# Pairs of nodes and hyperedges in 64 fixed steps on four engines

## Chip, core and metric

The kernel runs on one core of one Trainium2 chip. A core has a matrix engine (TensorE, "PE" in the profile, its weight loads "PEld"), three engines for elementwise work (VectorE "DVE", ScalarE "ACT", GpSimd "POOL") and SyncE ("SP"), which issues transfers. The engines run side by side, each in the order of its own queue, and wait for one another through semaphores. The metric is the time of the kernel on the device in microseconds (us). Before the change it is 2083.43 us, the median of three runs (2079.95 to 2089.01).

## What is computed

Four graph layers on x of 8 batches, 2048 nodes and 64 features, each of the form x = x + layer(relu(layer_norm(x))). The change lies in the first one, a hypergraph attention over 64 hyperedges. Cut to the part that matters:

```python
beta   = sigmoid((h @ a_gn)[:, None, :] + (agg @ a_ge)[:, :, None])
all_he = beta[..., None] * h[:, None, :, :] + (1.0 - beta[..., None]) * agg[:, :, None, :]
all_he = elu(all_he)                         # for every batch, hyperedge and node
coefs1 = softmax(where(H > 0, se, NEG))      # over the hyperedges of a node
g      = einsum('bne,benf->bnf', coefs1, all_he)
```

H says which hyperedge holds which node. It is sparse, so the kernel computes the mixture only for the pairs of a node and a hyperedge that exist. Afterwards g and a second candidate ("industry", made from the adjacency matrix earlier) are weighted against each other and added to x. Layers 1 to 3 follow, with products of the 2048 x 2048 adjacency.

## The kernel before

The function `layer0` first makes normalised features, tables of the hyperedges and the industry product, then the **pair stage** (L1115 to L1204), then the weighting of the two candidates (from L1210 on, called the *closing stage* below). `Layer1` and `Layers23` come after it.

The pair stage goes through 16 tiles of 128 nodes. A tile has up to 512 slots for pairs (`SLOTS`), taken as `NB` = 4 blocks of 128. So there are 64 blocks, and each handles all 8 batches at once: 128 pairs x 512 columns (8 batches x 64 features).

`begin(i)` (L1120) prepares tile i. ScalarE and VectorE make `sT`, ones and zeros that say which slot belongs to which node (L1125, L1126). A product with `Q` gives `px`, and a comparison on VectorE gives `oT`, which slot belongs to which hyperedge (L1130). Four transposes of `sT` on TensorE land in `pts`, and ScalarE copies them to `S` (L1133, L1135). Twelve small products `pm` (16 columns, L1140 to L1142) and two ScalarE operations give `be` (the gate) and `wt` (the weight) of every pair.

`pairs_of(i, k)` (L1149) handles block k. TensorE makes `pd` with three products and `pa` with one. VectorE makes `mix` = (be + 1) * pd (L1162) and adds `pa` (L1165). ScalarE takes an exponential into `ex` (L1166). VectorE combines the two (L1167), GpSimd multiplies by `wt` (L1168), and TensorE sums the pairs of a node into `pgs` (L1169, a float32 product that the profile counts as two instructions).

`end(i)` (L1171) divides by the sum of the weights on VectorE (`gn`, L1173), transposes back on TensorE (`ptg`, L1177) and stores the result from ScalarE in `gT`, whose buffer is called `hn` (L1179).

The features of a tile (`hhi` and `hlo`, 264 KB each) are loaded by GpSimd's queue two tiles ahead (`features`, L799 and L800). In tiles 0 to 11 that queue also issues one load of 1 MB of the adjacency (`aT`, L1918).

What sets the order: the kernel is written in a framework with a planner, which arranges the instructions of each engine by a simulated time of its own. In the pair stage nothing is pinned, so the planner's order holds. Elsewhere an instruction can be pinned behind the one traced before it on its engine: `InOrder(tc, engine)` (L622) does so for every call through it, and `kit.mm` and `kit.turn` (L724, L730) do it while `kit.strict` is set.

In layer 1, `scores` (L1447) loads rows `R` that VectorE needs in `attend`; the load is issued by SyncE's queue (L1453).

Of the kernel before, what the change touches and what calls it, by code (L numbers as in the profile page):

```python
# [8 lines left out]
FP = mybir.dt.float32  # L9
FR = mybir.dt.float32r  # L10
AF = mybir.ActivationFunctionType
OP = mybir.AluOpType
# [4 lines left out]
P = 128  # L17
B, N, F = 8, 2048, 64
E = 64
NP = B // 2  # L20
NT = N // P
# [10 lines left out]
def cols(c, w=CW):  # L32
    return slice(c * w, (c + 1) * w)
# [583 lines left out]
SLOTS, NB = 512, 4  # L617
HN = N // 2
# [16 lines left out]
class Kit:  # L635
# [88 lines left out]
    def mm(self, *args, **kw):  # L724

        one = self.nc.tensor.matmul(*args, **kw)  # L726
        if self.strict:
            self.tc.keep_in_program_order(one)

    def turn(self, dst, src):  # L730

        one = self.nc.tensor.transpose(dst, src, self.ident)
        if self.strict:
            self.tc.keep_in_program_order(one)
# [27 lines left out]
def layer0(kit, hn, x1_dram, open_early, late_tile, between):  # L762
# [5 lines left out]
    tc, nc, t = kit.tc, kit.nc, kit.t  # L768
    mm = nc.tensor.matmul
    ident, ones, bad = kit.ident, kit.ones, kit.bad  # L770
# [6 lines left out]
    neg1 = w0.tile([P, 1], FP, name="neg1")  # L777
# [8 lines left out]
    Q = lst.tile([P, NT, 2, E], FR, name="Q")  # L786
    slot = lst.tile([P, SLOTS], FP, name="slot")
    mid = lst.tile([P, NT], FP, name="mid")
    width = lst.tile([P, NT], FP, name="width")
    tab = lst.tile([P, B, F], FR, name="tab")  # L790
    ntab = lst.tile([P, B, F], FR, name="ntab")
    etab = lst.tile([P, 2 * B], FR, name="etab")
    rden = lst.tile([P, NT, B], FP, name="rden")

    def features(i):

        hi = lst.tile([P, B * F + 2 * B], FR, tag="hhi", name="hhi", bufs=3)
        lo = lst.tile([P, B * F + 2 * B], FR, tag="hlo", name="hlo", bufs=3)
        nc.gpsimd.dma_start(out=hi, in_=hi_dram[i].bitcast(FR))  # L799
        nc.gpsimd.dma_start(out=lo, in_=lo_dram[i].bitcast(FR))  # L800
        return hi, lo

    with ExitStack() as sA:
# [78 lines left out]
        with ExitStack() as s1:  # L882
            pool = s1.enter_context(tc.tile_pool(name="rank", bufs=1, reuse_waits="tile"))
            sb = s1.enter_context(tc.tile_pool(name="nf_sb", bufs=2, reuse_waits="tile"))
            ps = s1.enter_context(tc.tile_pool(name="nf_ps", bufs=2, space=PSUM, reuse_waits="tile"))
# [28 lines left out]
        with ExitStack() as s1:  # L914
            sp = s1.enter_context(tc.tile_pool(name="streamf", bufs=6, reuse_waits="tile"))
            sb = s1.enter_context(tc.tile_pool(name="e_sb", bufs=2, reuse_waits="tile"))
            ps = s1.enter_context(tc.tile_pool(name="e_ps", bufs=1, space=PSUM, reuse_waits="tile"))
# [4 lines left out]
            pg = ps.tile([P, B, F], FP, tag="pg", name="pg")  # L922
# [171 lines left out]
            last = None  # L1094
# [18 lines left out]
    gT = hn  # L1113
    with ExitStack() as s0:

        hot = s0.enter_context(tc.tile_pool(name="s_hot", bufs=2, reuse_waits="tile"))
        sb = s0.enter_context(tc.tile_pool(name="s_sb", bufs=2, reuse_waits="tile"))
        ps = s0.enter_context(tc.tile_pool(name="s_ps", bufs=1, space=PSUM, reuse_waits="tile"))

        def begin(i):  # L1120
            hi, lo = loaded.pop(0)

            sT = hot.tile([P, SLOTS], FR, tag="sT", name="sT")
            tmp = hot.tile([P, SLOTS], FP, tag="tmp", name="tmp", bufs=1)
            nc.scalar.activation(tmp, slot, AF.Abs, bias=mid[:, i : i + 1])  # L1125
            nc.vector.tensor_scalar(sT, tmp, width[:, i : i + 1], None, op0=OP.is_lt)  # L1126
            px = ps.tile([P, SLOTS], FP, tag="px", name="px", bufs=2)
            mm(px, Q[:, i].rearrange("p h e -> p (h e)"), sT, start=True, stop=True)
            oT = hot.tile([P, SLOTS], FR, tag="oT", name="oT")
            nc.vector.tensor_tensor(oT, px, slot, op=OP.is_equal)  # L1130
            pt = ps.tile([P, NB, P], FP, tag="px", name="pts", bufs=2)
            for k in range(NB):
                nc.tensor.transpose(pt[:, k, :], sT[:, k * P : (k + 1) * P].bitcast(FP), ident)  # L1133
            S = sb.tile([P, NB, P], FP, tag="S", name="S")
            nc.scalar.copy(S, pt)  # L1135

            pm = ps.tile([P, NB, 2 * B], FP, tag="px", name="pm", bufs=2)
            for k in range(NB):
                ks = slice(k * P, (k + 1) * P)
                mm(pm[:, k, :], sT[:, ks], hi[:, B * F :], start=True, stop=False)  # L1140
                mm(pm[:, k, :], sT[:, ks], lo[:, B * F :], start=False, stop=False)
                mm(pm[:, k, :], oT[:, ks], etab, start=False, stop=True)  # L1142
            be = sb.tile([P, NB, B], FP, tag="be", name="be")
            wt = sb.tile([P, NB, B], FP, tag="wt", name="wt")
            nc.scalar.activation(be, pm[:, :, 0:B], AF.Tanh, scale=0.5)
            nc.scalar.copy(wt, pm[:, :, B:])
            return hi[:, 0 : B * F], lo[:, 0 : B * F], sT, oT, S, be, wt

        def pairs_of(i, k, pg, hi, lo, sT, oT, S, be, wt):  # L1149
            ks = slice(k * P, (k + 1) * P)  # L1150
            flat = lambda a: a.rearrange("p b f -> p (b f)")
            pd = ps.tile([P, B, F], FP, tag="pd", name="pd", bufs=2)
            mm(flat(pd), sT[:, ks], hi, start=True, stop=False)
            mm(flat(pd), sT[:, ks], lo, start=False, stop=False)
            mm(flat(pd), oT[:, ks], flat(ntab), start=False, stop=True)
            pa = ps.tile([P, B, F], FP, tag="pa", name="pa", bufs=2)
            mm(flat(pa), oT[:, ks], flat(tab), start=True, stop=True)
            mix = sb.tile([P, B, F], FP, tag="mix", name="mix", bufs=3)
            ex = sb.tile([P, B, F], FP, tag="ex", name="ex", bufs=3)


            nc.vector.scalar_tensor_tensor(  # L1162
                mix, be[:, k, :, None].to_broadcast([P, B, F]), 1.0, pd, op0=OP.add, op1=OP.mult
            )
            nc.vector.tensor_tensor(mix, mix, pa, op=OP.add)  # L1165
            nc.scalar.activation(ex, mix, AF.Exp, bias=neg1)  # L1166
            nc.vector.scalar_tensor_tensor(ex, mix, 1.0, ex, op0=OP.max, op1=OP.min)  # L1167
            nc.gpsimd.tensor_tensor(mix, ex, wt[:, k, :, None].to_broadcast([P, B, F]), op=OP.mult)  # L1168
            return lambda: mm(flat(pg), S[:, k, :], flat(mix), start=k == 0, stop=k == NB - 1)  # L1169

        def end(i, pg):  # L1171
            gn = sb.tile([P, B, F], FP, tag="gn", name="gn")
            nc.vector.tensor_tensor(gn, pg, rden[:, i, :, None].to_broadcast([P, B, F]), op=OP.mult)  # L1173
            pt = ps.tile([P, NP, P], FP, tag="px", name="ptg", bufs=2)
            gf = gn.rearrange("p b f -> p (b f)")
            for p in range(NP):
                nc.tensor.transpose(pt[:, p, :], gf[:, p * P : (p + 1) * P], ident)  # L1177
            for p in range(NP):
                nc.scalar.activation(gT[p][:, i * P : (i + 1) * P], pt[:, p, :], AF.Identity, bias=neg1)  # L1179

        now = begin(0)

        for p in range(1, NP):
            nc.sync.dma_start(out=x1_dram[p], in_=t["xT"][p])
        late = None
        for i in range(NT):
            pg = ps.tile([P, B, F], FP, tag="pg", name="pgs")
            todo = []
            for k in range(NB):
                todo.append(pairs_of(i, k, pg, *now))  # L1190
                if k == 1 and i + 1 < NT:
                    after = begin(i + 1)
                if k == 2:
                    if i + 2 < NT:
                        loaded.append(features(i + 2))
                    load_early(i)
                if k == 1 and late is not None:
                    late()
                if k > 0:
                    todo[k - 1]()  # L1200
            todo[-1]()
            now = after
            late = lambda i=i, pg=pg: end(i, pg)
        late()  # L1204

    sP.close()
    one = between(None)
# [90 lines left out]
class Layer1:  # L1298
# [148 lines left out]
    def scores(self, p, hf, b2):  # L1447

        self.turn += 1
        r = (self.sb2 if self.turn % 3 == 0 else self.R).tile([P, HN], FP, tag="R", name="R", bufs=2 - (self.turn % 3 == 0))  # L1450
        if b2 is None:
            return r
        self.kit.nc.sync.dma_start(out=r, in_=self.r_dram[p, b2 : b2 + 1, cols(hf, HN)].to_broadcast([P, HN]))  # L1453
        return r

    def attend(self, aT, p, hS, vd, wd, hf, between):
# [98 lines left out]
class Weave:  # L1555
# [9 lines left out]
    def step(self, c):  # L1565
        d = next(c[1], None)
        if d is None:
            self.chains.remove(c)
        else:
            c[0] = self.now + d  # L1570
# [419 lines left out]
```

## Time and profile before

| | us |
|---|---|
| median of three runs | 2083.43 |
| profiled execution, its own time | 2082.92 |
| its span in the profile | 2081.0 |
| up to the pair stage | 0 to 246 |
| pair stage | 246 to 442.3 |
| closing stage of layer 0 | 442.3 to 521 |
| layer 1 | 521 to 938 |
| layers 2 and 3 | 938 to 2081 |

The profiled execution took 1.9 us more than its span and 0.5 us less than the median of the runs. Over the span TensorE is busy 96%, VectorE 58%, ScalarE 22% and GpSimd 13%. These are averages over stages with different limits. Busy time of TensorE also counts the draining of each product, so that a busy TensorE can still have room.

In a timeline or table of groups, a line gives the line of the kernel, engine, operation, the tile written and those read, and after the bar (or in square brackets) the idle time before it and what ended it.

### The profile page before, as it was taken

What the parts mean: (1) busy time and instruction counts of PE and PEld (TensorE: products, weight loads), DVE (VectorE), ACT (ScalarE), POOL (GpSimd) and SP (SyncE); (2) the same over time, 40 slices, a digit from 0 to 9 for tenths busy, and PEclk for the clock granted to TensorE, in tenths of its full rate; (3) what the DMA queues carried; (4) which work ended last, traced back from release to release, by engine and by line L of the source; (5) the groups of instructions that cost most, each with busy time, mean ns of one, the idle gap of its engine ahead of it and who ended that gap; (6) DMA issues with size and microseconds to landing.
All of it is one profiled execution on the core that took longest, in us unless ns stands there. A gap on an engine that the chain in (4) does not pass through costs nothing.

```text
span 2081.0 us, 23594 instructions
## 1 busy us (share of the span) xinstructions
PE 2005.6 (96%) x9164; PEld 1154.1 (55%) x9164; DVE 1196.8 (58%) x1882; ACT 455.5 (22%) x859; POOL 264.2 (13%) x383
## 2 busy tenths in 40 slices
PE   7999899887999999999999999999999999999997
PEld 4777655533322222227775557765477755577653
DVE  6667478976888888883224653225632156522355
ACT  4321244457112121112121111211111211112100
POOL 0211054422000000000001210002100012100022
PEclk9999899999999999999999999999999999999999
DMA  6666272157111111213200012101022000121000
GB/s 180 195 193 190 67 239 80 43 154 162 46 42 35 49 33 23 60 31 89 66 31 21 25 37 60 58 7 35 18 64 61 26 22 25 37 75 46 8 14 12
DMA packets 84251, 138.16 MB, mean 66 GB/s; under 512 B 32753, under 2 KB 33009, under 8 KB 81457
## 3 DMA queue, kind: packets, MB, share of 16 engines
q1 hardware_dynamic: 65200, 83.86, 13.7%
q0 software_dynamic: 18928, 52.70, 10.2%
q8 instruction: 74, 1.21, 0.2%
q14 instruction: 49, 0.39, 0.1%
HBM read 102.64 MB, written 37.03 MB: 67 GB/s over the span
## 4 chain that ended last, share of the span: by engine, by line
PE 68%; issue 15%; DVE 6%; POOL 4%; DMA 3%; ACT 2%; SPq 0%; POOLq 0%; DVEq 0%; ACTq 0%
PE acc L726 27%; PE o L726 11%; PE u L726 6%; PE dn L726 5%; PE acc L940 3%; PE pgs L1169 2%; PE var L726 2%; PE mean L726 2%; PE py L726 2%; POOL fold L1878 1%; DVE ex L1167 1%; DMA at<-in_adjT 1%; PE ph L726 1%; POOL ot L1879 1%; DMA iv<-ind_dram 1%
## 5 line engine op out<-in xcount | busy, mean ns | idle before, releaser
L726 PE MATMUL acc<-aT,parts 128*128 128x512 f32 x1664 | 456.0, 420 | 0.0
L726 PEld LDWEIGHTS acc<-aT,parts 128*128 128x128 f32 x1664 | 307.8, 188 | 111.8 <-issue 49.4
L1866 DVE TENSOR_TENSOR pr<-u,embf 128x512 f32<-128x512 f32 x256 | 170.7, 688 | 138.8 <-PE u L726 131.9
L1485 DVE SCALAR_TENSOR_TENSOR pt<-R,wd,aT 128x1024 f32<-128x1024 f32 x192 | 236.5, 1279 | 20.4 <-PE dn L726 6.6
L726 PE MATMUL u<-W3f,y 64*128 64x512 f32 x1024 | 241.0, 589 | 0.0
L726 PE MATMUL o<-pt,hS 128*64 128x512 f32 x1024 | 236.4, 599 | 3.0 <-DVE pt L1485 3.0
L726 PEld LDWEIGHTS u<-W3f,y 64*128 64x128 f32 x1024 | 99.2, 187 | 120.6 <-issue 120.6
L726 PEld LDWEIGHTS o<-pt,hS 128*64 128x64 f32 x1024 | 68.0, 136 | 161.4 <-issue 149.9
L940 PE MATMUL acc<-at,Y 128*128 128x512 f32 x512 | 137.0, 413 | 2.4 <-DVE ev L949 2.4
L726 PE MATMUL u<-W3f,v 64*128 64x512 f32 x512 | 138.8, 619 | 0.0
L726 PE MATMUL dn<-pt,vd 128*32 128x512 f32 x1024 | 123.1, 598 | 0.0
L1702 DVE TENSOR_TENSOR yb<-py,cb_f 128x512 f32<-128x512 f32 x32 | 22.1, 691 | 173.7 <-PE py L726 173.7
L1878 POOL TENSOR_TENSOR fold<-fold 128x256 f32<-128x256 f32 x64 | 47.7, 745 | 548.4 <-DVE fold L1877 510.6
L940 PEld LDWEIGHTS acc<-at,Y 128*128 128x128 f32 x512 | 95.8, 195 | 25.7 <-issue 4.3
L726 PE MATMUL acc<-aTl,parts 128*128 128x512 f32 x384 | 103.2, 405 | 0.0
L1870 DVE TENSOR_TENSOR pr<-pr 128x512 f32<-128x512 f32 x128 | 88.1, 688 | 2.2
L1485 DVE SCALAR_TENSOR_TENSOR pt<-R,wd,aTl 128x1024 f32<-128x1024 f32 x64 | 79.8, 1282 | 11.4 <-PE dn L726 8.2
L726 PEld LDWEIGHTS acc<-aTl,parts 128*128 128x128 f32 x384 | 72.2, 188 | 21.5 <-issue 5.7
L1169 PE MATMUL pgs<-mix,S 128*128 128x512 f32 x128 | 69.8, 635 | 13.1 <-POOL mix L1168 12.4
L1852 ACT COPY xs<-px 128x128 f32<-128x128 f32 x64 | 17.1, 267 | 272.7 <-POOL ot L1880 210.3
L1168 POOL TENSOR_TENSOR mix<-ex,wt 128x512 f32<-128x512 f32 x64 | 66.7, 1042 | 76.7 <-DVE ex L1167 66.4
L1770 POOL TENSOR_TENSOR bq<-bq,xp 128x512 f32<-128x512 f32 x16 | 20.5, 1283 | 434.1 <-DVE xp L1768 395.5
(321 smaller groups left out, 2672.8 us busy)
## 6 DMA issues: line engine op xcount, KB each, us to landing
at<-in_adjT POOLq DMA_DIRECT2D x32, 512.0 KB, 4.6
raw<-in_adjT SPq DMA_DIRECT2D x64, 256.0 KB, 3.4
aT<-in_adjT POOLq DMA_DIRECT2D x12, 1024.0 KB, 6.1
xp<-xd SPq DMA_DIRECT2D x45, 256.0 KB, 3.2
R<-r_dram SPq DMA_DIRECT2D x14, 512.0 KB, 3.8
hi_dram<-hi SPq DMA_DIRECT2D x16, 264.0 KB, 2.4
lo_dram<-lo SPq DMA_DIRECT2D x16, 264.0 KB, 3.4
hhi<-hi_dram POOLq DMA_DIRECT2D x16, 264.0 KB, 3.0
```

What stands on the lines that cost most here:

```text
L726: one = self.nc.tensor.matmul(*args, **kw)
L940: mm(acc[p], Y[h][:, m, p, :], at[:, k, :], start=m + h == 0, stop=m == NT - 1 and h == 1)
L1167: nc.vector.scalar_tensor_tensor(ex, mix, 1.0, ex, op0=OP.max, op1=OP.min)
L1168: nc.gpsimd.tensor_tensor(mix, ex, wt[:, k, :, None].to_broadcast([P, B, F]), op=OP.mult)
L1169: return lambda: mm(flat(pg), S[:, k, :], flat(mix), start=k == 0, stop=k == NB - 1)
L1485: nc.vector.scalar_tensor_tensor(pt, R[b2], wd[:, m, b2 : b2 + 1], aT[m][:, s].bitcast(FP), op0=OP.max, op1=OP.mult)
L1702: nc.vector.tensor_tensor(yb, py, bias[:, None, :].to_broadcast([P, 4, P]), op=OP.add)
L1770: nc.gpsimd.tensor_add(bq, bq, xp)
L1866: nc.vector.tensor_tensor(a, u[h], emb[:, i, 8 * w : 8 * w + 8, None].to_broadcast([P, 8, F]), op=OP.mult)
L1870: nc.vector.tensor_add(pr[h], pr[h], a)
L1878: nc.gpsimd.tensor_add(fold[:, :, 0:2, :], fold[:, :, 0:2, :], fold[:, :, 2:4, :])
L1879: nc.gpsimd.tensor_add(ot, fold[:, :, 0, :], fold[:, :, 1, :])
```

## The change

The pair stage is written anew. The parts of `begin`, `pairs_of` and `end` become small functions. A loop of 64 + 7 steps calls them so that each operation is written two or more steps behind its operands. VectorE, ScalarE, GpSimd and TensorE are pinned to the order of the text in this loop.

Apart from the order:

- the comparison that makes `sT` moves from VectorE to GpSimd;
- the four transposes of `sT` become products with a copy of the identity (`ident_r`) in the type that TensorE takes rounded (float32r), as `sT` is;
- more buffers: `sT` 3 instead of 2, `S` 3 instead of 2, `mix` 6 instead of 3, `ex` 4 instead of 3, and `pgs` in PSUM 2 instead of 1;
- in layer 1, the loads of `R` for the last pair of batches are pinned behind what was traced before them on SyncE's queue.

```diff
+        V, A, G = InOrder(tc, nc.vector), InOrder(tc, nc.scalar), InOrder(tc, nc.gpsimd)
...
-            nc.vector.tensor_scalar(sT, tmp, width[:, i : i + 1], None, op0=OP.is_lt)
+            G.tensor_scalar(d["sT"], tmp, width[:, i : i + 1], None, op0=OP.is_lt)
...
-                nc.tensor.transpose(pt[:, k, :], sT[:, k * P : (k + 1) * P].bitcast(FP), ident)
+                mm(d["pt"][:, k, :], d["sT"][:, k * P : (k + 1) * P], ident_r, start=True, stop=True)
...
+        for step in (nodes, ranks, edges, turn, turned, shares, shared):
+            step(0)
+        nodes(1)
...
+        for j in range(last + 7):
+            i, k = divmod(j, NB)
+            there = i + 1 < NT
+            if j < last:
+                pairs_of(j)
+            if k == 2 and i + 2 < NT:
+                nodes(i + 2)
+            if 1 <= j <= last:
+                mixed(j - 1)
+            if 3 <= j < last + 3:
+                weighed(j - 3)
+            if 5 <= j < last + 5:
+                gathered(j - 5)
+            if k == 0:
+                if there:
+                    ranks(i + 1)
+                if i > 2:
+                    done(i - 3)
+            if k == 1:
+                if there:
+                    turn(i + 1)
+                    edges(i + 1)
+                if i > 1:
+                    divided(i - 2)
+            if k == 2:
+                if there:
+                    turned(i + 1)
+                    shares(i + 1)
+                if i + 2 < NT:
+                    loaded.append(features(i + 2))
+                if i < NT:
                     load_early(i)
+                if i > NT:
+                    back(i - 2)
+                    done(i - 2)
+            if k == 3:
+                if 1 < i <= NT:
+                    back(i - 2)
+                if there:
+                    shared(i + 1)
...
+        if p == NP - 1:
+
+            self.kit.tc.keep_in_program_order(one)
```

The functions by engine: `nodes` makes `sT` (ScalarE, GpSimd). `ranks` makes `px` (TensorE) and `edges` makes `oT` (VectorE). `turn` writes `pts` (TensorE) and `turned` copies it to `S` (ScalarE). `shares` makes `pm` (TensorE), and `shared` makes `be` and `wt` (ScalarE). `mixed` holds the two VectorE operations and the exponential of a block. `weighed` is the third VectorE operation and GpSimd's product, `gathered` the sum into `pgs`. `divided`, `back` and `done` are the three parts of `end`.

## The prediction

> **What bounds the kernel now.** I read the stages first: busy time of each engine in five stretches of the span. Columns: stretch, its length, busy us (and instructions) of PE, PEld, DVE, ACT, POOL, then TensorE's granted clock, DMA share, GB/s.
>
> ```profile
> 246.00:442.30 196.30, 173.83 (x724) 111.58 (x726) 163.87 (x244) 84.76 (x191) 87.27 (x103) 0.95 0.36 111
> 442.30:521.00 78.70, 65.44 (x263) 24.41 (x260) 53.04 (x80) 56.37 (x77) 14.99 (x19) 0.95 0.83 198
> ```
>
> The pair stage takes 196.3 us with TensorE and VectorE both near 85% busy; the rest of the kernel hardly concerns the change. Successive starts of `gn`, once per tile, run from 273.9 to 439.2 us: 165.3 / 15 = 11.02 us per tile, 11.42 in the middle. Four tiles there (362.81 to 408.49 us) I took apart by groups, shapes separate:
>
> ```profile
> L1169 PE MATMUL pgs<-mix,S 128*128 128x512 f32 x32 | 17.4, 625 | 4.7 <-POOL mix L1168 4.5
> L1168 POOL TENSOR_TENSOR mix<-ex,wt 128x512 f32<-128x512 f32 x16 | 16.7, 1043 | 14.9 <-DVE ex L1167 14.8
> L1167 DVE SCALAR_TENSOR_TENSOR ex<-mix,ex 128x512 f32<-128x512 f32 x16 | 14.1, 879 | 3.8 <-ACT ex L1166 3.8
> L1165 DVE TENSOR_TENSOR mix<-mix,pa 128x512 f32<-128x512 f32 x16 | 10.9, 681 | 0.3
> L1162 DVE SCALAR_TENSOR_TENSOR mix<-be,pd 128x512 f32<-128x512 f32 x16 | 10.9, 681 | 0.1
> L1126 DVE TENSOR_SCALAR sT<-tmp,width 128x512 fp32r<-128x512 f32 x4 | 2.9, 715 | 0.0
> ```
>
> VectorE idles only 5.0 us of 45.68 (3.8 + 0.3 + 0.1 + 0.8 before `oT`), so it is occupied (45.68 - 5.0) / 4 = 10.17 us per tile. TensorE waits for GpSimd's product, GpSimd for VectorE's `ex`, VectorE for ScalarE's exponential: one block's chain, walked with little else to do. The waits of the same stretch, longest first, say it directly (columns: total us, times, longest):
>
> ```profile
> POOL mix L1168 <- DVE ex L1167: 14.8, 12, 3.0
> PEld pgs L1169 <- POOL mix L1168: 9.0, 10, 1.4
> ```
>
> Two timelines give the real pitch. A busy VectorE starts an operation every 0.60 us though each lasts 0.68, but 0.71 behind one whose result it reads (here 367.74 to 368.45):
>
> ```profile
> 367.74 0.68 DVE L1162 SCALAR_TENSOR_TENSOR mix<-be,pd 128x512 f32<-128x512 f32 x1
> 368.45 0.69 DVE L1165 TENSOR_TENSOR mix<-mix,pa 128x512 f32<-128x512 f32 x1
> 369.06 0.69 DVE L1167 SCALAR_TENSOR_TENSOR ex<-mix,ex 128x512 f32<-128x512 f32 x1
> 369.66 0.68 DVE L1162 SCALAR_TENSOR_TENSOR mix<-be,pd 128x512 f32<-128x512 f32 x1
> 370.26 1.22 DVE L1167 SCALAR_TENSOR_TENSOR ex<-mix,ex 128x512 f32<-128x512 f32 x1
> ```
>
> The last line is an `ex` that took 1.22 us: GpSimd's product ran then. On TensorE:
>
> ```profile
> 384.14 0.39 PE L1154 MATMUL pd<-hlo,sT 128*128 128x512 f32 x1
> 384.37 0.39 PE L1155 MATMUL pd<-ntab,oT 128*128 128x512 f32 x1
> 384.60 1.02 PE L1169 MATMUL pgs<-mix,S 128*128 128x512 f32 x2
> 385.06 0.80 PE L1157 MATMUL pa<-tab,oT 128*128 128x512 f32 x1
> 385.69 0.39 PE L1153 MATMUL pd<-hhi,sT 128*128 128x512 f32 x1
> ```
>
> A product of 512 columns costs 0.23 us, a `pgs` that needn't wait 385.69 - 384.60 - 0.23 = 0.86 us.
>
> **What the Trainium skill says.** GPSIMD Engine Reference, 1. Specifications: GpSimd's SBUF interfaces are shared with VectorE, with "contention with DVE instructions in a 2-port perf mode or with two SBUF inputs". The trace agrees: `ex`, with two SBUF inputs, has mean 879 and up to 1700 ns, the operations that read PSUM stay at 681. The same page, 3.1, gives 769 ns for a 512-element loop with one input on GpSimd; no such row is in this trace. Perfetto Trace Analysis, Identifying the Most-Contended Engine: matmul busy share is no measure of distance to the limit; hence the pitches above. TensorE: Matmul & The Clock Gate, Part 1: half clock after an idle window; the trace shows 0.56 from 256 to 267 us.
>
> **The change part by part.** VectorE per tile: `sT` leaves (0.72). What stays is 4 x (0.71 + 0.60 + 0.60) + `oT` 0.60 + `gn` 0.60 = 8.84 us. Holds by GpSimd are now (879 - 682) x 4 = 0.79. In the new order GpSimd's product (1.04) starts as `ex` ends, and VectorE's next `ex` comes 1.31 us later, behind two operations that read PSUM, so they should hardly meet; bounds 8.84 to 9.63.
>
> TensorE per tile: 16 x 0.23 = 3.68; `pgs` 4 x 0.86 = 3.44; `px` 0.23; twelve `pm` 1.34 (382.49 to 383.83 us); `ptg` 0.44 (376.41 to 376.85). Sum 9.13. `pts` as rounded products isn't in the trace: as cheap as now, 0.44, or each as dear as a 512-column product, 0.92. So 9.57 to 10.05; I take 9.8, in the middle.
>
> GpSimd per tile: 4 x 1.04 + two or three DMA issues of 0.57 + `sT`. For that I take an estimate of 0.8 us from the skill's 769 ns; bounds 0.5 (an iota of 512 took 0.55) and 1.3 (the 512-wide addition of L1770). Sum about 6.7, no bound. `sT` stands two steps, some 5 us, before the `px` that reads it; with ScalarE's part its chain is 1.5 us long. On GpSimd only the product of the same step is queued behind it. ScalarE: 4 x 0.73 + 1.14 + 0.59 + 0.72 + 0.38 = 5.75, no bound.
>
> So TensorE sets the pace. Does something else stop it? With TensorE at 2.5 us a step, VectorE starts step j when `pd` of j-1 is written, 1.0 us into TensorE's step j-1. So the `ex` of block j-5, VectorE's third operation of step j-2, ends 1.0 + 1.9 = 2.9 us after TensorE began step j-3, and GpSimd's product 1.2 later. TensorE asks for it 0.9 us into step j, 3 x 2.5 + 0.9 = 8.4 us after that beginning. Some 4 us are spare, which also cover the 2.2 to 2.7 us that GpSimd's queue now loses before some `hhi` loads. The tightest are the two PSUM buffers shared by `px`, `pts`, `pm` and `ptg`: `turn` waits for four ScalarE copies written one step before, with some 1.8 us spare. For uneven steps (the one with `pm` 1.3 us longer, VectorE's with `oT` and `gn` 1.2) and semaphores I add an estimated 0.3. Tile: 10.1 us.
>
> Stage: the first `mix` starts at 251.9 us now; GpSimd's slower `sT` and the identity copy add about 1: 253. Then 63 steps x 10.1 / 4 = 159.1. The clock dip stays: 10.3 us busy at 0.56 lose 4.5. Drain behind the last `mix`: 1.31 + 0.73 + 0.69 + 1.05 + 1.25 + 0.69 + 0.44 + 1.14 + waits 0.5 = 7.8. End at 424.4 instead of 442.3: 17.9 us less.
>
> After it everything moves along. At 442 three accumulating stores (1 MB each) and seven `iv` loads fill the transfers, and one `iv` lands 18.7 us late; they start when the last tile is done and its buffers are free, in both kernels. More buffers change only which tile `iv` overlays: nothing, give or take 3.
>
> R: at 831 us three loads (512 KB each) go out together, and VectorE waits 0.80 and 1.22 us for two of them. Pinned, the third goes later, behind the two loads `xp` that SyncE issues at 836.7 us and one that follows them; its rows are needed only in the second half of that pair, half of 836 to 938 us on; two share the transfers. Between 0 and 2 us gained, I take 1.
>
> Sum: 17.9 + 1 = 19 us from the profiled 2082.9: 2064; the median of the runs stood 0.5 higher: 2064.5.
>
> **Rivals.** *VectorE and GpSimd still collide* (holds of 0.8 plus waits in the tight PSUM ring): tile near 10.85, 63 / 4 x 10.85 = 170.9, 11.8 more than mine: 2076. For it: VectorE's slack against TensorE is under 1 us; against: ten of fourteen operations read PSUM.
>
> *Slower: the fixed order makes GpSimd's operations fall on every `ex`.* `sT` and the DMA issues push the product back until it covers the next `ex`; a hold has cost up to 1.70 - 0.69 = 1.0. Four per tile: 9.2 + 4.0 = 13.2, 63 / 4 x 3.1 = 49 us over mine: 2113. It decides from 2.7 us of holds per tile on: 9.2 + 2.7 = 11.9, the stage is then 10 us longer than now. Against: the alternation mends itself, as a late product delays TensorE, not `ex`.
>
> *The gain is swallowed in the closing stage*: the planner issues `iv` or the stores in a worse order; the stretch with DMA share 0.83 is 78.7 us long, a tenth of it lost is 8: 2073.
>
> *Better still*: the dip of the clock goes as well, and 9.6 per tile: 4.5 + 7.9 less, 2052.
>
> **How the numbers follow.** Mine 0.66 (own range 2055 to 2074), collision 0.14, slower 0.11, swallowed 0.06, better 0.03. Runs of this kernel spread by 0.4%, so 0.5% (10.4 us) is what can be told from no change: faster means under 2073. Faster takes mine, better and half of swallowed, less a margin: 0.75; same 0.15 (collision); slower 0.10. The range 2053 to 2084 leaves out the slower case, its own lower end apart, and a part of better.
>
> **What would show it.** `gn` every 10.1 us; hardly any wait of `pgs` for GpSimd; mean `ex` below 750 ns; no `sT` on VectorE, a GpSimd row of 0.5 to 1.3 us; `pts` starting 0.11 to 0.23 us apart; the stage over by 424; the closing stage still 79 us. Wrong if the waits of TensorE move to `pts` or `px` (the PSUM ring), if `ex` stays near 880, or if a step waits for GpSimd's queue behind an `hhi` load.

## The result and the profile after

The changed kernel takes 2055.03 us (median of 4 runs, 2053.27 to 2057.83), the kernel before 2086.22 us in the same session. The ratio is 0.9857, with a 95% interval of 0.9834 to 0.9881. Forecast were 2064.5 us and a range of 2053 to 2084. The profiled execution took 2053.27 us, its span 2051.2; before these were 2082.92 and 2081.0.

To see where the 29.8 us of span went, I cut both spans at the same events. The first column ends where VectorE makes the reciprocal degrees just ahead of the pair stage, the second with the last copy to `hn`, the third with the first `pt` of layer 1, the fourth with its last `ds`.

| us | up to the pair stage | pair stage | closing stage | layer 1 | layers 2 and 3 |
|---|---|---|---|---|---|
| before | 244.7 | 197.7 | 78.6 | 417.3 | 1142.7 |
| after | 241.7 | 169.1 | 82.3 | 415.2 | 1142.9 |
| difference | -3.0 | -28.6 | +3.7 | -2.1 | +0.2 |

So the pair stage gave nearly everything. The first and third columns also move where no edit reaches: over the kernels below, with the same code ahead of the pair stage, the first runs from 235.4 to 250.6 us, and the closing stage, where its code is that of the changed kernel, from 79.1 to 86.1. So the 3.0 us less and the 3.7 us more are within what these stages scatter. The pair stage repeats: three traces with the same code in it (the changed kernel and two of those below) give 169.1 us each. I judge edits by it.

The stages by busy time, after (same columns as before: stretch, length, PE, PEld, DVE, ACT, POOL, granted clock, DMA share, GB/s):

```profile
246.00:410.50 164.50, 160.16 (x718) 112.21 (x719) 148.77 (x228) 82.35 (x190) 112.21 (x117) 0.97 0.44 131
410.50:495.40 84.90, 68.76 (x272) 25.88 (x269) 54.35 (x82) 58.65 (x81) 15.34 (x19) 0.92 0.82 189
```

TensorE is now busy 160.2 of 164.5 us. Four tiles in the middle, 282.34 to 320.68 us, take 38.34 us, so 9.58 each. Their groups:

```profile
L630 POOL TENSOR_TENSOR mix<-ex,wt 128x512 f32<-128x512 f32 x16 | 17.0, 1063 | 4.6 <-DVE ex L630 4.4
L726 PE MATMUL pgs<-mix,S 128*128 128x512 f32 x32 | 16.3, 592 | 0.0
L630 DVE SCALAR_TENSOR_TENSOR ex<-mix,ex 128x512 f32<-128x512 f32 x17 | 12.7, 749 | 0.0
L630 DVE TENSOR_TENSOR mix<-mix,pa 128x512 f32<-128x512 f32 x17 | 11.7, 688 | 1.8
L630 POOL TENSOR_SCALAR sT<-tmp,width 128x512 fp32r<-128x512 f32 x5 | 7.8, 1560 | 0.0
```

Pinned operations all carry the helper's line, L630 or L726, and are told apart by their tiles. The 4.7 us that `pgs` stood idle in four tiles are now 0.0. VectorE's 3.8 us ahead of `ex` are 0.0, and GpSimd's wait for `ex` fell from 14.8 to 4.4. `sT` on GpSimd takes 1.56 us, twice what I had taken.

What changed shows best in the chain, followed back to what released each piece (columns: start, length, what). One block of the kernel before goes from engine to engine:

```profile
363.40 0.63 ACT ex L1166
364.05 1.71 DVE ex L1167
365.90 1.05 POOL mix L1168
366.99 1.12 PE pgs L1169 x2
```

After, a whole tile is TensorE alone, and the next tile begins where it ends:

```profile
291.92 1.24 PE pm L726 x12
293.16 0.79 PE pd L726 x3
293.95 0.23 PE pa L726
294.18 0.86 PE pgs L726 x2
295.04 0.44 PE ptg L732 x4
295.48 0.69 PE pd L726 x3
...
297.26 0.23 PE px L726
297.49 0.69 PE pd L726 x3
...
299.28 0.39 PE pts L726 x4
299.67 0.76 PE pd L726 x3
...
301.51 1.24 PE pm L726 x12
```

From 340 us on a tile takes 9.85, and the piece that grew is the one whose buffers I had called the tightest. The chain again, then the waits of 340.12 to 379.53 us (total, times, longest):

```profile
357.35 0.64 PE pts L726 x4
```

```profile
PEld pts L726 <- ACT hn L630: 3.3, 4, 0.8
```

`pts` takes 0.64 instead of 0.39, since it waits for ScalarE's copies of the tile before to free the PSUM buffer. That costs 0.27 us in each of five tiles, 1.3 us in all.

### The profile page after: what moved, and what is told of

Same layout as the page of the kernel before. It is cut to its first block, busy times and chain, and to the rows that moved or that the text cites. A ratio compares the mean times of both kernels' runs of the same rounds, so it can differ in the third digit from the quotient of the medians.

```text
span 2051.2 us, 23618 instructions
## 1 busy us (share of the span) xinstructions
PE 1992.0 (97%) x9164; PEld 1153.7 (56%) x9164; DVE 1184.3 (58%) x1867; ACT 454.4 (22%) x859; POOL 291.4 (14%) x399
## 3 DMA queue, kind: packets, MB, share of 16 engines
q1 hardware_dynamic: 65200, 83.86, 13.9%
## 4 chain that ended last, share of the span: by engine, by line
PE 71%; issue 15%; POOL 4%; DVE 3%; DMA 3%; ACT 2%; SPq 0%; POOLq 0%; DVEq 0%; ACTq 0%
PE acc L726 28%; PE o L726 11%; PE dn L726 6%; PE u L726 6%; PE pd L726 3%; PE acc L940 3%; PE pgs L726 2%; PE var L726 2%; PE mean L726 2%; PE py L726 2%; POOL fold L1964 1%; DMA iv<-ind_dram 1%; PE pm L726 1%; POOL ot L1965 1%; PE ph L726 1%
## 5 line engine op out<-in xcount | busy, mean ns | idle before, releaser
L726 PE MATMUL acc<-aT,parts 128*128 128x512 f32 x1664 | 456.0, 419 | 0.0
L726 PEld LDWEIGHTS acc<-aT,parts 128*128 128x128 f32 x1664 | 307.8, 188 | 111.8 <-issue 49.4
L726 PE MATMUL u<-W3f,y 64*128 64x512 f32 x1024 | 241.0, 589 | 0.0
L726 PE MATMUL o<-pt,hS 128*64 128x512 f32 x1024 | 236.4, 599 | 0.8 <-DVE pt L1571 0.6
L726 PEld LDWEIGHTS u<-W3f,y 64*128 64x128 f32 x1024 | 99.2, 187 | 120.6 <-issue 120.6
L726 PEld LDWEIGHTS o<-pt,hS 128*64 128x64 f32 x1024 | 68.0, 136 | 159.2 <-issue 150.2
L726 PE MATMUL u<-W3f,v 64*128 64x512 f32 x512 | 138.8, 619 | 0.0
L726 PE MATMUL dn<-pt,vd 128*32 128x512 f32 x1024 | 123.1, 598 | 0.0
L726 PE MATMUL acc<-aTl,parts 128*128 128x512 f32 x384 | 103.1, 405 | 0.0
L726 PEld LDWEIGHTS acc<-aTl,parts 128*128 128x128 f32 x384 | 72.2, 188 | 21.5 <-issue 5.7
L630 POOL TENSOR_TENSOR mix<-ex,wt 128x512 f32<-128x512 f32 x64 | 68.3, 1069 | 33.7 <-DVE ex L630 28.9
L726 PEld LDWEIGHTS dn<-pt,vd 128*32 128x32 f32 x1024 | 26.7, 108 | 80.8 <-issue 75.4
```

Of the source, the lines that this page charges most:

```text
L630: self.tc.keep_in_program_order(getattr(self.engine, name)(*args, **kw))
```

## The experiments

My theory, A in the records, is that the gain comes from distance: each engine finds its operands ready since they were asked for steps ago, and a fixed order keeps it so. The rivals credit one part instead, such as the comparison moved off VectorE, the extra buffers or the products in place of transposes. Not everything stands two steps behind its operands, as the section on the change has it: `mix` is one step behind `pd`, the exponential stands in the step of its sum, and GpSimd's product in that of its `ex`. Two steps lie between the exponential and `ex`, and two between the product and `pgs`. The measured stage lengths stand against 169.1 us of the changed kernel and 197.7 us of the kernel before.

**The shortest distance**: `ex` stands in the step of its exponential, and the sum one step later.

```diff
-            if 3 <= j < last + 3:
-                weighed(j - 3)
-            if 5 <= j < last + 5:
-                gathered(j - 5)
+            if 1 <= j < last + 1:
+                weighed(j - 1)
+            if 2 <= j < last + 2:
+                gathered(j - 2)
```

> The kernel after, with ex combined in the same step as its exponential is asked for and the sum into pgs one step later. Everything else of the change stays (pins, buffers, sT on GpSimd, pts as products). Theory A: VectorE now waits some 0.8 us for ScalarE in each of 64 steps, a step takes near 3.0 us and a tile 13.0, so the stage is about 50 us longer: 2095 to 2110. Theory B: VectorE's work is as small as in the kernel after, 2054 to 2065.

Measured: 2110.56 us, ratio to before 1.0124 (1.0095 to 1.0154), pair stage 225.4 us. With every other edit in place, the shorter distance costs 56 us and makes the kernel slower than the one before. VectorE's timeline shows what comes back (start, length, engine, line, operation, and in brackets the idle time before it):

```profile
322.01 0.69 DVE L630 SCALAR_TENSOR_TENSOR ex<-mix,ex 128x512 f32<-128x512 f32 x1 [0.86 <-ACT ex L630]
322.62 0.68 DVE L630 SCALAR_TENSOR_TENSOR mix<-be,pd 128x512 f32<-128x512 f32 x1
323.40 0.69 DVE L630 TENSOR_TENSOR mix<-mix,pa 128x512 f32<-128x512 f32 x1
324.94 0.69 DVE L630 SCALAR_TENSOR_TENSOR ex<-mix,ex 128x512 f32<-128x512 f32 x1 [0.85 <-ACT ex L630]
```

VectorE stands 0.85 us in every block for the exponential of its own last sum. A block takes it 324.94 - 322.01 = 2.93 us, and with `oT` and `gn` a tile takes 4 x 2.93 + 2 x 0.6 = 12.9 us. Starts of `gn` are 12.93 us apart up to 339 us and up to 13.9 later, where TensorE's clock dips. That is near the 13.2 of my slower rival, but by another mechanism: the rival had `ex` held by GpSimd, and here `ex` has a mean of 733 ns in 305 to 375 us.

**One step less for `ex`, two for the sum**

```diff
-            if 3 <= j < last + 3:
-                weighed(j - 3)
-            if 5 <= j < last + 5:
-                gathered(j - 5)
+            if 2 <= j < last + 2:
+                weighed(j - 2)
+            if 3 <= j < last + 3:
+                gathered(j - 3)
```

> The kernel after, with ex combined two steps behind pairs_of instead of three and the sum into pgs three steps behind instead of five. Theory A by its own count: some 4 us are spare, two steps less take 5 us of distance and VectorE's move gives 2.5 back, so 1 to 2 us stay spare: same time within 3 us, 2052 to 2058. If every step of distance is needed (GpSimd's queue with sT and loads delays products by more than that): pgs waits for mix again, 2060 to 2075.

Measured: 2052.64 us, 0.9863 (0.9825 to 0.9900), pair stage 169.3. There was slack to spare, as counted, but not much more: in 305 to 375 us `pgs` waits 1.3 us for GpSimd again. Here as at the shortest distance the sum stands one step behind the product. What differs is whether `ex` stands in the step of its exponential or one later, and that alone is worth 56 us.

**No pins.** The text, the distances and the buffers stay; the planner may arrange.

```diff
-        V, A, G = InOrder(tc, nc.vector), InOrder(tc, nc.scalar), InOrder(tc, nc.gpsimd)
+        V, A, G = nc.vector, nc.scalar, nc.gpsimd
...
-        kit.strict = True
         last = NB * NT
```

> The kernel after without any pin in the pair stage (the pin of R stays): text, buffers, sT on GpSimd and pts as products are those of the kernel after, the planner orders. Theory A: most of the gain goes, 2070 to 2085, with pgs waiting for GpSimd's mix as before. Theory B, or the buffers as the cause: the gain stays, 2053 to 2062.

Measured: 2061.77 us, 0.9895 (0.9868 to 0.9922), pair stage 172.6. Only 3.5 of 28.6 us go, as Theory B had it. The second half of my theory falls: a fixed order isn't needed for most of the gain, since the planner keeps close to a text in which operations already stand apart. What the pins still save shows where its tiles are slow (timelines of GpSimd, ScalarE and TensorE):

```profile
345.85 2.08 POOL L1134 TENSOR_SCALAR sT<-tmp,width 128x512 fp32r<-128x512 f32 x1
```

```profile
347.96 0.72 ACT L1133 ACTIVATE tmp<-slot,mid 128x512 f32<-128x512 f32 x1 [3.47 <-POOL sT L1134]
348.59 0.86 ACT L1234 ACTIVATE hn<-ptg,neg 128x128 f32<-128x128 f32 x3
```

```profile
350.37 0.66 PE L726 MATMUL pts<-ident_r,sT 128*128 128x128 f32 x4 [0.66 <-ACT hn L1234]
```

The planner has put the next tile's `tmp` right behind `sT`, whose one input buffer it overwrites. ScalarE stands 3.47 us, the copies to `hn` are queued behind it, and TensorE's `pts` waits for those. `pts` of five successive tiles starts at 328.98, 339.82, 350.37, 360.91 and 371.44 us: 10.6 us a tile where the changed kernel takes 9.9, which is 2.8 us over these four.

**The buffers alone, in the order of before** (`sT`, `S`, `mix`, `ex` and `pgs` get the numbers of the changed kernel):

```diff
-            mix = sb.tile([P, B, F], FP, tag="mix", name="mix", bufs=3)
-            ex = sb.tile([P, B, F], FP, tag="ex", name="ex", bufs=3)
+            mix = sb.tile([P, B, F], FP, tag="mix", name="mix", bufs=6)
+            ex = sb.tile([P, B, F], FP, tag="ex", name="ex", bufs=4)
```

> The kernel before with the buffer counts of the kernel after (sT 3, S 3, mix 6, ex 4, pgs 2) and nothing else. Theory A: the planner's order keeps the chains, at most 5 us are gained: 2077 to 2086. Theory C (buffers as the cause): 2055 to 2065.

Measured: 2073.09 us, 0.9963 (0.9952 to 0.9975), pair stage 187.4. Buffers alone give 10.3 of 28.6 us, between the theories. In 335 to 405 us `ex` falls from 869 to 686 ns, so it is no longer held; but `sT` on VectorE rises from 715 to 974 ns, and the wait of GpSimd for `ex` grows from 23.4 to 29.6 us. Freeing `ex` without the order leaves the chain of one block.

**The move of `sT` alone, in the order of before**

```diff
-            nc.vector.tensor_scalar(sT, tmp, width[:, i : i + 1], None, op0=OP.is_lt)
+            nc.gpsimd.tensor_scalar(sT, tmp, width[:, i : i + 1], None, op0=OP.is_lt)
```

> The kernel before with sT made on GpSimd and nothing else. Theory A: VectorE loses 0.7 us per tile, GpSimd gets 1.56 us in front of products that are waited for; between 5 us gained and 10 lost: 2077 to 2093. Theory B: 0.7 us x 16 = 11 us or more gained: 2060 to 2072.

Measured: 2094.93 us, 1.0065 (1.0046 to 1.0084), pair stage 207.6. That is a little beyond what Theory A allowed. The edit that helps in the new order costs 9.9 us in the old one. GpSimd's timeline, TensorE's and the busy time of the 4 us that follow tell why (the last with the columns of the stages above):

```profile
355.61 2.12 POOL L1126 TENSOR_SCALAR sT<-tmp,width 128x512 fp32r<-128x512 f32 x1
357.63 0.59 POOL L800 DMA_DIRECT2D hlo<-lo_dram  x1
358.24 1.06 POOL L1168 TENSOR_TENSOR mix<-ex,wt 128x512 f32<-128x512 f32 x1
```

```profile
359.36 1.61 PE L1169 MATMUL pgs<-mix,S 128*128 128x512 f32 x2 [2.22 <-POOL mix L1168]
```

```profile
359.40:363.40 4.00, 4.00 (x9) 2.67 (x10) 2.58 (x4) 1.33 (x3) 1.50 (x2) 0.57 0.18 54
```

The product's `ex` was ready at 356.33 us, but the product starts at 358.24, queued behind `sT` and a load. TensorE stands 2.22 us for it, and in the 4 us after that its clock is 0.57: the delay is paid twice. It happens once per tile from 345 to 414 us, six times in all, with waits of 2.21 to 2.24 us.

**The order and the buffers alone, and each of the other two edits with them.** `sT` back on VectorE:

```diff
-            G.tensor_scalar(d["sT"], tmp, width[:, i : i + 1], None, op0=OP.is_lt)
+            V.tensor_scalar(d["sT"], tmp, width[:, i : i + 1], None, op0=OP.is_lt)
```

> The kernel after, with sT made on VectorE again. Theory A (the distance between an operation and its operands lets TensorE run without waits; TensorE's own products set the pace): VectorE has about 9.2 of 9.6 us per tile in use and takes 0.5 to 0.7 us back, so it comes to 9.7 to 9.9, about as long as TensorE's tile: 2054 to 2060 us, ex with a mean near 700 ns. Theory B (VectorE's load was the limit, and the gain is sT and the holds that leave it): 0.7 to 1.5 us per tile come back, 2065 to 2078 us.

Transposes in place of products:

```diff
-                mm(d["pt"][:, k, :], d["sT"][:, k * P : (k + 1) * P], ident_r, start=True, stop=True)
+                kit.turn(d["pt"][:, k, :], d["sT"][:, k * P : (k + 1) * P].bitcast(FP))
```

> The kernel after with pts as four transposes against the float32 identity again. Four starts of pts are 0.11 us apart in the kernel before; in the kernel after the group of four takes about 0.50 us to the next product against 0.44. Nothing measurable: within 2 us of the kernel after, 2052 to 2057. If the product form mattered as much as its upper bound in the prediction, 8 us faster.

Both of these edits at once:

> The kernel after with sT on VectorE and pts as transposes, as in the kernel before: only the order, the buffers and the pin of R are left of the change. The two single runs lost 4.1 and 3.6 us in the pair stage, both with longer waits at pts. If they add: 169.1 + 7.7 = 177 us; if both are the same wait: 173. In either case the order and its buffers carry 20 us or more of the 28.6: 2058 to 2068 in all. If the gain needs the three together: 185 us or more, 2072 and up.

| | time, us | ratio to before | pair stage, us | lost of 28.6 |
|---|---|---|---|---|
| `sT` on VectorE | 2062.37 | 0.9893 (0.9863 to 0.9923) | 173.2 | 4.1 |
| transposes | 2059.73 | 0.9909 (0.9889 to 0.9928) | 172.7 | 3.6 |
| both | 2060.35 | 0.9903 (0.9876 to 0.9931) | 172.7 | 3.6 |

Both single runs fell outside what I had put first (2054 to 2060 and 2052 to 2057). Order and buffers give 25.0 of 28.6 us without the other two edits. Each of those is worth nothing without the other, and together they are worth 3.6. The chains show why: with `sT` on VectorE it is VectorE, not TensorE, that carries the chain through the middle of the stage (here with `sT` on VectorE and the products kept).

```profile
331.53 0.60 DVE ex L630
332.13 0.60 DVE oT L630
...
333.25 0.48 DVE sT L630
333.72 0.61 DVE mix L630
```

Eight tiles there take 81.2 us: two take 9.56 each, the other six 10.35 on average. By the prediction's own count VectorE needs 8.84 + 0.72 = 9.56 with `sT`, and `ex` at a mean of 854 ns, where I had put it near 700, adds (854 - 682) x 4 = 0.69. So the edits to TensorE's work can't help there. With the transposes and `sT` on GpSimd, TensorE starts with the same 9.58 us and then, in five tiles, takes 10.30; the chain passes ScalarE's copies:

```profile
357.15 0.72 ACT ex L630
357.87 1.03 ACT hn L630 x4
...
358.95 0.66 PE pts L732 x4
```

This is the PSUM ring again, only worse than in the changed kernel. Why transposes make it worse isn't settled: where nothing waits, four of them and the three `pd` behind them take 0.44 + 0.69 us in the chain, the products and their `pd` 0.39 + 0.76, which is the same.

**The PSUM wait taken away.** The copies to `hn` are placed ahead of the step's exponential:

```diff
+            if k == 0 and i > 2:
+                done(i - 3)
             if 1 <= j <= last:
                 mixed(j - 1)
...
-                if i > 2:
-                    done(i - 3)
```

> The kernel after, with done (the four ScalarE copies out of ptg) ahead of the exponential in the steps with k = 0; in the last steps nothing changes. In the kernel after the tiles from 340 us on wait 0.7 us each at pts for these copies and take 9.85 us, those from 282 to 321 us don't and take 9.59. Theory A with the shared PSUM buffers as what is left: that wait goes, all tiles near 9.6, 2 to 4 us less in the pair stage (167 us or less, from the comparison of VectorE's rdeg to the last copy, against 169.1). If the wait has another cause, it stays. The whole kernel: 2050 to 2056.

Measured: 2055.03 us, 0.9868 (0.9842 to 0.9894), pair stage 168.6. The wait of `pts` is gone and tiles stay at 9.58 to 9.69 us. The stage shrinks by 0.5 us, less than the 1.3 that five tiles had lost and far less than the 2 to 4 on record, and the whole time doesn't move. The cause of the wait was the one named, its size small.

**The pin on `R` taken away**

```diff
-        if p == NP - 1:
-
-            self.kit.tc.keep_in_program_order(one)
```

> The kernel after without the pin of the R loads in layer 1. From the two traces layer 1 took 417.3 us before and 415.2 after, so 2 us come back: 2055 to 2058, with three R loads at the start of the last pair. If the planner's shifted clock, not the pin, changed that place: no difference.

Measured: 2063.44 us, 0.9916 (0.9901 to 0.9931); layer 1 takes 416.3 us instead of 415.2. The three loads go out together again, at 797 us. Over layer 1 the waits for `R` are 6.4 us without the pin, 5.2 with it and 6.2 before. The other traces agree: layer 1 takes 414.6 to 415.4 us in the ten with the pin and 415.6 to 417.3 in the four without. So the pin is worth about 1 us. The whole time, beyond the range on record, can't show it: the profiled execution of this kernel took 2048.08 us and the timed ones 2062.7 to 2064.3, with the same pair stage of 169.1 us in the trace.

**The closing stage.** It is 3.7 us longer than before. Its chain passes one `iv` load; first the kernel before, then the changed one:

```profile
442.97 18.68 DMA iv<-ind_dram
```

```profile
411.88 20.93 DMA iv<-ind_dram
```

I took this load for the cause. It is not shown to be one. With `sT` on VectorE it takes only 18.24 us, and the stage 86.0. Nor do TensorE and ScalarE stand still meanwhile, as the record below has it: in these 20.9 us they are busy 17.5 and 13.6 us with other chunks (columns as in the stages above).

```profile
411.88:432.81 20.93, 17.46 (x60) 5.50 (x60) 13.99 (x19) 13.61 (x15) 1.41 (x2) 0.92 1.00 237
```

Three `iv` loads were fetched ahead of the end of the pair stage, and the three 1 MB stores placed later and pinned:

```diff
         first(0)
         kit.strict = False
         first(1)
+        for i in range(2, 5):
+            fetch(i)
...
-            if i in (1, 4, 8):
-                p = 1 + i // 4
-                nc.gpsimd.dma_start(out=x1_dram[p], in_=gT[p], accum_op=OP.add)
+            if i in (5, 9, 13):
+                p = i // 4
+                tc.keep_in_program_order(nc.gpsimd.dma_start(out=x1_dram[p], in_=gT[p], accum_op=OP.add))
```

> The kernel after, with two edits behind the pair stage: three of the iv loads are issued before the loads of xo, and the three 1 MB accumulating stores of hn stand at later places (steps 5, 9 and 13 of the closing stage instead of 1, 4 and 8) and are pinned there on GpSimd's queue. In the kernel after TensorE and ScalarE stand still from 412 to 433 us, until an iv load lands 20.9 us after its issue among those stores. If the stores are what delays it: it lands after some 5 us, the closing stage takes 65 to 70 us instead of 82, 2038 to 2045 in all. If the closing stage is bound by the sum of its transfers: no gain, 2050 to 2056.

The same together with the earlier copies to `hn`:

> The last two edits together (done ahead of the exponential; stores late): the gains add, 2036 to 2043. Nothing of the computation is left out.

Measured: 2050.41 us, 0.9853 (0.9827 to 0.9880), closing stage 77.0; and together 2053.76 us, 0.9871 (0.9847 to 0.9895), closing stage 77.2. The longest `iv` piece left in the chain is this:

```profile
420.68 2.72 DMA iv<-ind_dram
```

The load of 20.9 us is gone from the chain, the stage only 5 us shorter (2 us below the shortest of the others), well under the gain on record in both runs. The waits of that stage in the first of the two kernels:

```profile
POOL aTl L2010 <- DVE iv L630: 27.0, 1, 27.0
...
PEld pf L726 <- ACT th_s L630: 14.0, 16, 5.2
...
PEld pd L726 <- DVE iv L630: 11.4, 14, 1.5
```

The second and third are waits of TensorE for ScalarE and VectorE, chunk by chunk, and the changed kernel had them too (11.9 and 12.6 us): beside the load ran a chain that is nearly as long. GpSimd's 27.0 us ahead of an `aTl` load were 24.5 in the changed kernel; what they cost isn't isolated. No version here is shown to beat the changed kernel: the intervals of all the near ones overlap with its own.

Not tried: the new order with the old buffers. Buffers alone gave 10.3 us and order and buffers 25.0, so the order adds 14.7 on top of them; what it is worth without them stays open.

## Why the prediction was right or wrong

Direction, mechanism and bound were right: TensorE sets the pace, the chain of one block is gone, and the time lies in the range. The gain was under-sized, 29.8 us of span against 19. That 2055.03 us still falls at the very edge of my own range (2055 to 2074) is partly luck: the drain and the scatter of the closing stage took back 6.1 us of what the steps gave beyond my sum. By the prediction's own terms:

| term | forecast, us | measured, us | effect on the end |
|---|---|---|---|
| first `mix` | 253 | 250.3 | -2.7 |
| 63 steps and the clock dip | 159.1 + 4.5 | 150.3 | -13.3 |
| drain behind the last `mix` | 7.8 | 10.2 | +2.4 |
| end of the pair stage | 424.4 | 410.8 | -13.6 |
| closing stage | 78.6 | 82.3 | +3.7 |
| layer 1 | -1 | -2.1 | -1.1 |

**The tile is where it was mis-sized.** I took TensorE's work as 9.8, the middle of 9.57 to 10.05, and added 0.3 for uneven steps and semaphores. Measured were 9.58 in the first half and 9.85 later. The chain of a tile above gives the terms: `pm` 1.24 (forecast 1.34), `ptg` 0.44, `px` 0.23, `pgs` 4 x 0.86, all products `pd` and `pa` 3.86 (3.68) and `pts` 0.39 (0.44 to 0.92). So the rounded `pts` are no dearer than the transposes had been, and taking the middle put 0.2 too much. The allowance of 0.3 was the larger error: TensorE took its uneven steps without a wait, since its operands lay ready. The 0.5 us too many per tile make 63 / 4 x 0.5 = 7.9 us, as the rival *better still* had it.

**The clock dip** I put down as staying at 256 to 267 us, during the steps, with 4.5 us lost. It is now at 246 to 256 (clock 0.52); in 256 to 267 the clock is 1.00. Part of it lies ahead of the first `mix` at 250.3. Behind it TensorE is busy some 4.6 us at half clock, an estimated loss of 2.3 us. So about half of the 4.5 us went, which that rival had let go whole. I had given it 0.03; its 2052 is the nearest figure to what was measured.

**The number of full steps** was wrong too. From the first `mix` on, four steps have no `pgs` yet, those of the first two tiles have no `ptg`, and the last four steps prepare no further tile. By the terms above that is 4 x 0.86 + 2 x 0.44 + 0.23 + 0.39 + 1.24 = 6.2 us, an estimate, of work that my 63 full steps counted and the loop doesn't contain. These items together are more than the 13.3; what stands against them, such as the waits of `pts` and of the first steps, isn't taken apart.

**The first `mix`** came earlier only because the part ahead of it was 3.0 us shorter in this execution, by chance. Counted from the start of the stage it comes 8.6 us in, against 7.2 before, so the fill is 1.4 longer where I had said 1.

**The drain** was too short by 2.4 us. GpSimd's last three products stand in one row; this is its timeline:

```profile
402.81 3.81 POOL L630 TENSOR_TENSOR mix<-ex,wt 128x512 f32<-128x512 f32 x3 [0.95 <-DVE ex L630]
```

They take 1.27 us each where I had 1.05, and the last one ends 1.9 us after its `ex`. The other half lies with VectorE: the last `ex` starts 3.2 us after the last `mix`, where my sum has 2.0, since two other `ex` and a `gn` stand ahead of it. With no new blocks between them, the distance of the loop is of no use there.

**VectorE and GpSimd.** `ex` has a mean of 749 ns in the four tiles at 9.58, as forecast, but 853 in 305 to 375 us. So `ex` and GpSimd's product do meet, which I had thought would hardly happen. The collision is not gone, it has only lost its weight: VectorE's spare time takes it. What the Trainium skill, GPSIMD Engine Reference, 1. Specifications, says of shared interfaces agrees with the trace, as before: the two operations that read PSUM stay at 678 and 688 ns. The same page's 3.1 gives the 769 ns as the best case of a tight loop and names no instruction. As a measure for `sT` it failed: 1.56 us here and 2.12 in the old order, outside my bounds of 0.5 to 1.3. The measurement decides. It did no harm because GpSimd had room: 31.6 us busy of 38.3 in those four tiles. In the old order the same error would have mattered, as the run with `sT` moved alone shows.

**The tightest place** was named rightly, the two PSUM buffers of `px`, `pts`, `pm` and `ptg`, but the 1.8 us spare were too many: the wait is there from 340 us on, at 0.27 us per tile.

**The closing stage** was to stay as it was, give or take 3; it grew by 3.7, within the scatter of that stage, and no cause is shown. **The pin on `R`** was right: about 1 us by the run without it. The other 1 us in layer 1 has no edit behind it.

**The rivals.** *Collision* and *slower* ask for holds of `ex` that delay TensorE; `pgs` has 0.0 us of idle time. *Slower* meets its price by coincidence, 2110.6 us against 2113, at the shortest distance only, and there by VectorE's waits for the exponential. *Swallowed* asks for a longer closing stage; its 3.7 us are within the scatter.

## What to carry to other kernels

When a chain of short operations over several engines is the bound, write each operation far enough behind its operands in the text that no engine waits for a result just asked for, with the buffers for it; here one step between the exponential and `ex` against none decided 56 us, the pins 3.5. Then add up the bound engine's own pitches over the steps that really occur, and add no allowance where the other engines have room. Judge a move of work between engines in the order in which it will run: the same move cost 9.9 us in the old order and gained 4.1 in the new one, and there only together with another small edit that was worth nothing alone.

## What was not expected of the hardware

- A comparison with a scalar per partition, 128x512 from float32 to the rounded type, takes 1.56 us on GpSimd, and 1.9 and 2.1 on average in two other orders. On VectorE it takes 0.48 us in the new order, and on average 0.72 in the middle of the old one and 0.97 there with more buffers.
- In the run with `sT` moved alone, each of the six waits of 2.2 us on TensorE, in the middle of dense work, was followed by some 4 us near half clock; in the one shown, products of 512 columns came every 0.43 instead of 0.23 us. Two waits of 1.5 us in that run were not followed by a dip, and of eight waits of 1.9 us at the shortest distance four were. Over 270 to 400 us the granted clock is 1.00 before and after, but 0.95 with `sT` moved alone and 0.93 at the shortest distance. The kernel before waits too, but at most 1.0 us at a time in that stretch. So in these runs long single waits were paid again in the clock, short ones were not.
- Four rounded products with an identity took 0.39 us in the chain and four transposes 0.44, but the three `pd` behind the products took 0.76 instead of 0.69.
